# Copies of v and tau in DRAM: 16 KB apart instead of 4 KB

## The chip, the cores and the metric

The kernel runs on one core of a Trainium2 chip. The metric is the device time of one execution in microseconds; the time given for a kernel is the median of its runs. A core has five engines that work side by side, each with an instruction queue of its own: PE (TensorE, matrix products; PEld is its loading of weights), DVE (VectorE), ACT (ScalarE), POOL (GpSimd) and SP (SyncE, which here issues every DMA). DMAs move data between DRAM (HBM) and the on-chip memory SBUF; 16 DMA engines carry them. Everything is in 32-bit floats.

## The reference, cut to what matters

An image batch `x` of 4 x 64 channels x 256 x 256 goes through four layers. Layers 0, 2 and 3 are long convolutions with separable filters that small networks make; layer 1 works on Haar coefficients, and it alone uses `v` and `tau`:

```python
def conv_layer(x, ...):                    # layers 0, 2, 3
    hx, hy = filter_net_x(z), filter_net_y(z)
    y = causal_conv2d(x, outer(hx, hy))    # by FFT in the reference
    return y + x * bias

def layer_1(x, v, conv_w, tau):            # v, tau: (2, 1, 1, 256, 256)
    f1 = haar2d(x)
    acc = 0
    for i in range(2):
        f3 = f1 * v[i]
        f4 = einsum('bchw,oc->bohw', f3, conv_w[i])
        acc += sign(f4) * relu(abs(f4) - tau[i])
    return haar2d(acc, inverse=True) + x
```

A value of `v[i]` or `tau[i]` belongs to one place of the 256 x 256 coefficients and is the same for all 64 channels and all images.

## The kernel before

The kernel works on two groups of two images. Phase A is layer 0 and the forward Haar transform; it leaves the coefficients in the DRAM tensors `coef`. Phase B is the mixing of layer 1; it reads `coef`, and leaves its result in `mixed`. Phase C is the inverse Haar transform and layers 2 and 3. The phases are interleaved: phase A of group 0 runs alone, phase A of group 1 beside phase B of group 0, phase C of group 0 beside phase B of group 1, and phase C of group 1 alone.

Phase B runs in 64 steps per group. In a step the 128 partitions are 2 halves of 64 channels, and each half holds 2 rows of coefficients (`W = 2 * N = 512` values). The tiles for `v` and `tau` hold for each partition both branches `i` (2 x 512 values, 4 KB), and within a half all 64 channels hold the same values. So a load spreads one 4 KB row over 64 partitions. The kernel keeps `COPIES = 8` copies of every such row in DRAM, and each copy is read by 8 partitions:

```python
COPIES = 8
...
    taus = dram.tile([C, 2, COPIES, 2, W], F32, tag="taus", name="taus")
...
        def load(s):                                   # phase B, step s
            ...
            d["f"] = bp.tile([P, NB, W], F32, tag="ft", ..., bufs=4)
            for rows, f in step_of(coef[grp], s, d["f"]):      # 2 DMAs, 64 rows of 4 KB each
                nc.sync.dma_start(f, rows)
            for name, src in (("v", v), ("tau", taus)):
                t = d[name] = bp.tile([P, 2, W], F32, tag=name, ..., bufs=3)

                at = src.offset + s * 4 * W * COPIES
                flat = bass.AP(src.tensor, at, [[2 * W, 2 * COPIES], [0, C // COPIES], [1, 2 * W]])
                nc.sync.dma_start(t.rearrange("p e w -> p (e w)"), flat)
```

The source of a load is 16 rows (2 halves x 8 copies), each 4 KB after the one before it, each read 8 times. `v` is an input that is already laid out with its copies. `tau` is first scaled on the chip, and then written 8 times into the DRAM tensor `taus`:

```python
    def copy_tau(k):
        tau_sb = thresholds[1]                          # [128, 4, N] in SBUF
        for i in range(2):
            to = bass.AP(taus.tensor, taus.offset + (k * 2 + i) * W, [[2 * W * COPIES, P], [1, W]])
            nc.sync.dma_start(to, tau_sb[:, 2 * i : 2 * i + 2].rearrange("p h k -> p (h k)"))
...
    rest += [lambda k=k: copy_tau(k) for k in range(COPIES)]
```

`rest` is a list of preparations that is dealt out between the pieces of phase A of group 0; `copy_tau` comes last in it. In the same stretch SP issues, round by round, the images `x` of the next rounds and the filter matrices `tx` and `ty`:

```python
        def piece(t, j):                                # phase A, round t
            ...
            if j == 0:
                ...
                filters(t + 2)                          # tx, ty: 6 DMAs
            ...
                if j == 2 * BLOCKS + 1:
                    load(t + 2)                         # x: 1 MB, bufs=3
```

A step of phase B on one branch `i` goes through all the engines: PE makes the product `f` from `ft` and the mixing weights (L595), DVE multiplies it by `v` into `x` (L610), ACT takes the sign and the magnitude (L614, L618), DVE subtracts `tau` (L621) and applies the threshold (L624), and POOL adds to `gt` (L636 to L640), which is stored to `mixed` (L645).

Of the kernel before, what the change touches and what calls it, by code (L numbers as in the profile page):

```python
# [41 lines left out]
F32 = mybir.dt.float32  # L42
# [5 lines left out]
P = 128  # L48
B, C, N = 4, 64, 256
# [12 lines left out]

COPIES = 8

GROUPS = 2
NB = B // GROUPS
CI = 4 // NB
# [7 lines left out]
W = 2 * N  # L75
# [3 lines left out]

IMAGES = (GROUPS, NB, ROUNDS, CI, BLOCKS, ROW, N)  # L80
TO_ROUNDS = (0, 2, 1, 5, 3, 4, 6)
# [10 lines left out]
def conv_haar_kernel(  # L92
    ctx: ExitStack, tc: tile.TileContext, x, zT, w1, wbd, cols, decay, wo_first, decay_first, bias, forward, inverse, wcol, wrow, pack, v, tau, out
):
    nc = tc.nc
# [3 lines left out]
    dram = ctx.enter_context(tc.tile_pool(name="dram", bufs=1, space=DRAM))  # L99
# [3 lines left out]
    def coefficients(name):  # L103
        return dram.tile([CI, STEPS // 2, PAIR], F32, tag=name, name=name)

    coef = [coefficients(f"coef{g}") for g in range(GROUPS)]
    mixed = [coefficients(f"mixed{g}") for g in range(GROUPS)]
    filt = [dram.tile([P, REPEATS, PERIOD], F32, tag=f"filt{l}", name=f"filt{l}") for l in range(NL)]

    taus = dram.tile([C, 2, COPIES, 2, W], F32, tag="taus", name="taus")  # L110


    def pool(name, bufs, stack=ctx, **kw):
# [157 lines left out]
    def copy_tau(k):  # L271
        tau_sb = thresholds[1]
        for i in range(2):
            to = bass.AP(taus.tensor, taus.offset + (k * 2 + i) * W, [[2 * W * COPIES, P], [1, W]])
            nc.sync.dma_start(to, tau_sb[:, 2 * i : 2 * i + 2].rearrange("p h k -> p (h k)"))

    first_x = [load_x(0)]
    forward_sb = const.tile([P, ROW], F32, tag="forward", name="forward_sb")
# [15 lines left out]
    rest += [lambda l=l, q=q, k=k: spread(l, q, k) for l in (1, 2) for q in range(4) for k in thirds]  # L294
    rest.append(scale_tau)
    rest += [lambda k=k: copy_tau(k) for k in range(COPIES)]

    TILES = [(r, c) for r in range(2) for c in range(2)]
# [128 lines left out]
    def phase_a():  # L427


        total = GROUPS * ROUNDS  # L430
        st = [dict() for _ in range(total)]
# [97 lines left out]
    def phase_b(grp):  # L529
# [7 lines left out]
        def step_of(ap, s, images):  # L537

            n = NB * W
            by_e = images.rearrange("(m e) b w -> e m (b w)", e=CI)  # L540
            at = [ap.offset + (e * STEPS // 2 + s // 2) * PAIR + s % 2 * P // CI * n for e in range(CI)]
            return [(bass.AP(ap.tensor, at[e], [[n, P // CI], [1, n]]), by_e[e]) for e in range(CI)]

        def load(s):
            if s >= STEPS:
                return
            d = st[s]
            d["f"] = bp.tile([P, NB, W], F32, tag="ft", name=f"ft_{grp}_{s}", bufs=4)
            for rows, f in step_of(coef[grp], s, d["f"]):
                nc.sync.dma_start(f, rows)  # L550
            for name, src in (("v", v), ("tau", taus)):
                t = d[name] = bp.tile([P, 2, W], F32, tag=name, name=f"{name}_{grp}_{s}", bufs=3)

                at = src.offset + s * 4 * W * COPIES
                flat = bass.AP(src.tensor, at, [[2 * W, 2 * COPIES], [0, C // COPIES], [1, 2 * W]])
                nc.sync.dma_start(t.rearrange("p e w -> p (e w)"), flat)

        def four(name, at, b):
# [89 lines left out]
        def piece(u, j):  # L648

            s, i = divmod(u, 2)  # L650
            if j == 0:
                if u < units:
                    multiply(u)
                if 0 < u <= units:
                    less(u - 1)
                if 1 < u <= units + 1:
                    add(u - 2)
            elif j == 1:
                if u + 1 < units:
                    mix(u + 1)  # L660
                if u < units:
                    sign(u)
                if 0 < u <= units:
                    threshold(u - 1)
                if i == 0 and s > 0:
                    load(s + 2)
            else:
                if u < units:
                    magnitude(u)
                if i == 0 and s < STEPS:  # L670
                    exchange(s)
                if i and s > 0:

                    if s == 2:
                        part()
                        store(0)
                    if s > 1:
                        store(s - 1)

        def start():  # L680
            mixers.append(bp.tile([P, P], F32, tag="mix", name=f"mix_{grp}", bufs=1))
            nc.sync.dma_start(mixers[0], pack)
            for s in range(3):
                load(s)
# [7 lines left out]
    def phase_c():  # L692


        total = GROUPS * ROUNDS
        alone = total - ROUNDS
# [273 lines left out]
```

## Time and profile before

| what | value |
|---|---|
| time, median of 3 runs | 2849.76 us (2846.62 to 2851.04) |
| span of the profiled run | 2849.9 us |
| PE busy | 2429.2 us, 85% of the span |
| POOL busy | 1947.6 us, 68% |
| DVE busy | 1582.2 us, 56% |
| ACT busy | 1427.8 us, 50% |
| read from and written to HBM | 413.12 and 215.35 MB |

The profile is of one execution. Its page gives busy times by engine and in 40 slices, the chain of waits that ended last, the costliest groups of instructions by source line, and the DMA issues; the same trace can be asked for stretches of time. Lines such as L307 are lines of the kernel. `out<-in` names what an instruction or a DMA writes and reads: `v<-in_v` is the load of `v`, `tau<-taus` that of `tau`, `taus<-tau_sb` the writing of a copy. Two lines of the page show how the DMA engines' work is spread over the 40 slices of the span:

```profile
DMA  5668887989989998666888888887885444444432
GB/s 156 219 212 262 239 283 245 274 280 283 277 268 294 280 286 276 207 186 195 257 263 244 270 259 240 257 258 230 259 245 184 146 145 149 142 158 134 158 118 93
```

Each digit is the mean busy share of the 16 DMA engines in tenths in one slice of 71 us, and below it stands what they moved. Phase B of group 0 lies in slices 7 to 16, that of group 1 in slices 19 to 30.

### The profile page before, as it was taken

How to read it: one execution, taken by the hardware profiler on the slowest of the kernel's cores; microseconds unless marked ns; L12 is line 12 of the kernel's file. 1: busy time of each engine (PE TensorE's matmuls, PEld its weight loads, DVE VectorE, ACT ScalarE, POOL GpSimd, SP SyncE). 2: the span in 40 equal slices, each digit the busy share in tenths (PEclk: the TensorE clock that was granted, in tenths of full speed). 3: DMA queues.
4: the chain of work that ended last, by engine and by line, in shares of the span. 5: the costliest groups of instructions: out<-in, count | busy, mean ns of one | idle time of the engine just before them, and what ended most of it. 6: DMA issues, size and time to landing. Idle time of an engine off the chain costs nothing.

```text
span 2849.9 us, 120142 instructions
## 1 busy us (share of the span) xinstructions
PE 2429.2 (85%) x53276; PEld 1931.0 (68%) x53276; DVE 1582.2 (56%) x1779; ACT 1427.8 (50%) x2361; POOL 1947.6 (68%) x2422
## 2 busy tenths in 40 slices
PE   6999998667677676769888888888889999999999
PEld 5777776444444454547676767676667888888888
DVE  2353336777677777527776767676763333333333
ACT  1222224666656566426675666675763333333332
POOL 2787777977778787648777777776765555555561
PEclk9999999988988888879999999999999999999999
DMA  5668887989989998666888888887885444444432
GB/s 156 219 212 262 239 283 245 274 280 283 277 268 294 280 286 276 207 186 195 257 263 244 270 259 240 257 258 230 259 245 184 146 145 149 142 158 134 158 118 93
DMA packets 243773, 636.31 MB, mean 223 GB/s; under 512 B 43174, under 2 KB 125767, under 8 KB 227128
## 3 DMA queue, kind: packets, MB, share of 16 engines
q1 hardware_dynamic: 243256, 628.64, 71.5%
q8 instruction: 419, 6.86, 1.0%
q14 instruction: 98, 0.80, 0.1%
HBM read 413.12 MB, written 215.35 MB: 221 GB/s over the span
## 4 chain that ended last, share of the span: by engine, by line
PE 40%; DMA 23%; DVE 9%; ACT 5%; POOL 4%; issue 3%; SPq 3%; DVEq 0%; ACTq 0%; POOLq 0%
PE c1c L307 8%; PE c2r L307 8%; PE c2c L307 7%; PE c1r L307 6%; DMA ft<-coef 6%; DMA v<-in_v 4%; DMA tau<-taus 4%; PE f L595 3%; PE c0ps L319 3%; DMA x<-in_x 3%; DVE a L621 2%; DMA mixed<-gt 2%; DVE x L610 2%; DMA g<-mixed 2%; PE a2ps L307 1%
## 5 line engine op out<-in xcount | busy, mean ns | idle before, releaser
L392 POOL TENSOR_TENSOR i<-i,g 128x16 f32<-128x16 f32 x744 | 394.5, 550 | 489.3 <-ACT g L375 476.6
L595 PE MATMUL f<-ft,mix 64*64 64x512 f32 x2048 | 341.3, 687 | 262.2 <-DMA ft<-coef 180.5
L610 DVE TENSOR_TENSOR x<-f,v 128x1024 f32<-128x1024 f32 x256 | 312.0, 1219 | 267.0 <-PE f L595 140.4
L307 PEld LDWEIGHTS a1ps<-tx,x 64*64 64x64 f32 x8192 | 322.5, 142 | 121.5 <-issue 61.7
L307 PE MATMUL a1ps<-tx,x 64*64 64x192 f32 (+3 forms) x8192 | 354.2, 315 | 34.6 <-issue 11.2
L614 ACT ACTIVATE m<-x 128x1024 f32<-128x1024 f32 x256 | 272.0, 1063 | 209.9 <-DVE x L610 151.7
L307 PEld LDWEIGHTS c2r<-tx,cy 64*64 64x64 f32 x8192 | 307.6, 137 | 92.0 <-ACT ch L745 53.9
L307 PEld LDWEIGHTS c1c<-ty,ch 64*64 64x64 f32 x8192 | 300.9, 133 | 90.2 <-ACT ch L745 53.1
L307 PEld LDWEIGHTS a2ps<-ty,ay 64*64 64x64 f32 x8192 | 308.1, 140 | 70.8 <-issue 44.3
L307 PE MATMUL c2r<-tx,cy 64*64 64x256 f32 (+3 forms) x8192 | 341.6, 306 | 11.8 <-ACT ch L745 6.5
L307 PE MATMUL c1c<-ty,ch 64*64 64x192 f32 (+3 forms) x8192 | 330.3, 299 | 22.8 <-issue 12.7
L307 PE MATMUL a2ps<-ty,ay 64*64 64x256 f32 (+3 forms) x8192 | 340.8, 311 | 8.5 <-issue 7.8
L621 DVE TENSOR_TENSOR a<-a,tau 128x1024 f32<-128x1024 f32 x256 | 313.8, 1226 | 60.9 <-ACT a L618 60.5
L618 ACT ACTIVATE a<-x 128x1024 f32<-128x1024 f32 x256 | 264.8, 1034 | 162.3 <-DVE m L624 161.7
L307 PE MATMUL c1r<-tx,z 64*64 64x64 f32 (+3 forms) x8192 | 329.9, 302 | 12.5 <-ACT g L375 6.8
L307 PEld LDWEIGHTS c1r<-tx,z 64*64 64x64 f32 x8192 | 306.8, 136 | 49.8 <-issue 28.8
L636 POOL TENSOR_TENSOR gt<-gt,m 128x1024 f32<-128x1024 f32 x128 | 303.1, 2368 | 44.9 <-DVE m L624 41.8
L745 ACT COPY ch<-c1r 128x512 f32<-128x512 f32 x256 | 137.2, 588 | 390.5 <-PE c1r L307 390.1
L471 DVE SCALAR_TENSOR_TENSOR x<-x,bias_sb,a2ps 128x512 f32<-128x512 f32 x256 | 179.4, 742 | 268.2 <-PE a2ps L307 243.1
L307 PE MATMUL c2c<-ty,ch 64*64 64x192 f32 (+3 forms) x8192 | 319.3, 298 | 9.2 <-issue 9.2
L624 DVE SCALAR_TENSOR_TENSOR m<-a,m 128x1024 f32<-128x1024 f32 x256 | 313.0, 1223 | 22.1 <-DVE a L621 0.5
L307 PEld LDWEIGHTS c2c<-ty,ch 64*64 64x64 f32 x8192 | 300.5, 134 | 32.3 <-issue 18.4
(71 smaller groups left out, 3193.1 us busy)
## 6 DMA issues: line engine op xcount, KB each, us to landing
coef<-f SPq DMA_DIRECT2D x256, 256.0 KB, 4.1
ft<-coef SPq DMA_DIRECT2D x256, 256.0 KB, 6.8
v<-in_v SPq DMA_DIRECT2D x128, 512.0 KB, 7.5
tau<-taus SPq DMA_DIRECT2D x128, 512.0 KB, 8.5
mixed<-gt SPq DMA_DIRECT2D x256, 256.0 KB, 7.2
g<-mixed SPq DMA_DIRECT2D x256, 256.0 KB, 5.9
x<-in_x SPq DMA_DIRECT2D x63, 1024.0 KB, 8.5
out<-o SPq DMA_DIRECT2D x63, 1024.0 KB, 5.0
```

The source lines that it names most:

```text
L307: nc.tensor.matmul(ps[r][half(c), j % 2, k * ROW :], data[half(r), c, k, bass.ts(j, ROW)], t(r, c)[:, : N - k * ROW], start=k == 0, stop=k ...
L319: nc.tensor.matmul(ps[r][half(c)].rearrange("p h k -> p (h k)"), matrix[half(r)], pairs(r, c).rearrange("p h k -> p (h k)"), start=True, s ...
L392: engine.tensor_tensor(to, s, d, op)
L471: nc.vector.scalar_tensor_tensor(to, old, bias_sb[:, c : c + 1], ps, ALU.mult, ALU.add)
L595: nc.tensor.matmul(un[u]["f4"][half(q), b, :], mixers[0][half(r), bass.ts(i, C)], st[s]["f"][half(r), b], start=True, stop=True, tile_posi ...
L610: nc.vector.tensor_tensor(un[u]["x"], un[u]["f4"], both(u, "v"), ALU.mult)
L614: nc.scalar.activation(un[u]["m"], un[u]["x"], AF.Sign)
L618: nc.scalar.activation(un[u]["a"], un[u]["x"], AF.Abs)
L621: nc.vector.tensor_tensor(un[u]["a"], un[u]["a"], both(u, "tau"), ALU.subtract)
L624: nc.vector.scalar_tensor_tensor(un[u]["m"], un[u]["a"], 0.0, un[u]["m"], ALU.max, ALU.mult)
L636: nc.gpsimd.tensor_tensor(st[s]["g"], st[s]["g"], m, ALU.add)
L745: later(lambda y=y, ps=ps: nc.scalar.copy(y, ps))
```

## The change

The rows of four steps are put between two copies: `taus` and `v` go from (step, half, copy, row) to (step / 4, half, copy, step % 4, row). A load reads the same 16 rows as before, but they stand `FAR * 4 KB = 16 KB` apart. The aim is quicker loads of `v` and `tau`, by another placing of what the 16 DMA engines read at one time. `v` is laid out so before the launch. `taus` is written on the chip, and its rows no longer lie at one distance from partition to partition; so `copy_tau` writes every copy in 16 DMAs of 16 rows instead of 2 DMAs of 128 rows.

```diff
+FAR = 4
...
-    taus = dram.tile([C, 2, COPIES, 2, W], F32, tag="taus", name="taus")
+    taus = dram.tile([C // FAR, 2, COPIES, FAR, 2, W], F32, tag="taus", name="taus")
...
     def copy_tau(k):
         tau_sb = thresholds[1]
         for i in range(2):
-            to = bass.AP(taus.tensor, taus.offset + (k * 2 + i) * W, [[2 * W * COPIES, P], [1, W]])
-            nc.sync.dma_start(to, tau_sb[:, 2 * i : 2 * i + 2].rearrange("p h k -> p (h k)"))
+            n = FAR * 2 * W
+            for far in range(FAR):
+
+                for q in range(2):
+                    at = taus.offset + (q * COPIES + k) * n + (far * 2 + i) * W
+                    to = bass.AP(taus.tensor, at, [[2 * COPIES * n, C // FAR], [1, W]])
+                    rows = tau_sb[2 * far + q : P : 2 * FAR, 2 * i : 2 * i + 2]
+                    nc.sync.dma_start(to, rows.rearrange("p h k -> p (h k)"))
...
-                at = src.offset + s * 4 * W * COPIES
-                flat = bass.AP(src.tensor, at, [[2 * W, 2 * COPIES], [0, C // COPIES], [1, 2 * W]])
+                n = 2 * W
+                at = src.offset + (s // FAR * 2 * COPIES * FAR + s % FAR) * n
+                flat = bass.AP(src.tensor, at, [[FAR * n, 2 * COPIES], [0, C // COPIES], [1, n]])
...
-        "v": f(np.repeat(v[:, :, None], COPIES, axis=2)),
+
+        "v": f(np.repeat(v.reshape(C // FAR, FAR, 2, 2, W).transpose(0, 2, 1, 3, 4)[:, :, None], COPIES, axis=2)),
```

## The prediction

> **What bounds the kernel now.** I read the table by stage first, because the share of busy time on the page averages stages that have different limits. The stretches are: layer 0 of the first two images alone (370 to 420 us, a sample of it), mixing of group 0 beside layer 0 of group 1 (455 to 1150), mixing of group 1 beside layers 2 and 3 of group 0 (1290 to 2130), and layers 2 and 3 of group 1 alone (2130 to the end).
>
> ```profile
> core 0: us, PE busy (x) PEld busy (x) DVE busy (x) ACT busy (x) POOL busy (x), PEclk, DMA share, GB/s
> 370.00:420.00 50.00, 48.28 (x1166) 38.67 (x1158) 19.83 (x29) 13.90 (x26) 38.28 (x65) 1.00 0.79 279
> 455.00:1150.00 695.00, 491.43 (x8063) 319.08 (x8056) 514.40 (x488) 431.60 (x579) 547.07 (x607) 0.87 0.92 279
> 1290.00:2130.00 840.00, 724.41 (x15615) 579.40 (x15611) 595.54 (x601) 561.56 (x899) 623.33 (x639) 0.96 0.84 249
> 2130.00:2850.00 720.00, 706.06 (x18532) 628.26 (x18523) 248.46 (x352) 267.08 (x583) 381.05 (x525) 0.99 0.44 143
> ```
>
> In the first and last rows PE is busy 97 and 98% of the time: TensorE bounds them. In the row from 455 no engine is over 79% (POOL 547.07 of 695.00), but the 16 DMA engines are busy 92% of it: that stage is bound by transfers. In the row from 1290 PE has 86%, DMA 84%: a mixture. Only these two middle stages load v and tau. The chain of waits, asked for each of the two, says the same.
>
> ```profile
> by line: DMA ft<-coef 14.1%; DMA v<-in_v 14.0%; DMA x<-in_x 12.3%; DMA tau<-taus 12.1%; DVE x L610 5.1%; DVE a L621 5.1%; issue 4.5%; PE f L595 3.5%; DVE x L471 3.3%; DMA mixed<-gt 3.0%; PE a2ps L307 2.8%; DVE m L624 2.8%; DMA coef<-f 2.1%;
> ```
>
> ```profile
> by line: PE c1c L307 8.9%; DMA ft<-coef 7.9%; PE f L595 7.5%; PE c2r L307 7.5%; issue 6.1%; PE c2c L307 5.2%; DMA tau<-taus 5.0%; PE c1r L307 4.7%; DMA g<-mixed 4.6%; DMA mixed<-gt 4.3%; DMA v<-in_v 3.6%; DVE a L621 2.9%; DVE x L610 2.7%; A
> ```
>
> In the first line the DMA entries add to 57.6% of the stage (14.1 + 14.0 + 12.3 + 12.1 + 3.0 + 2.1), 26.1% of it v and tau themselves. In the second they add to 25.4% (7.9 + 5.0 + 4.6 + 4.3 + 3.6); much of the rest is PE. Next, the page's list of DMA issues, to see whether v and tau are slow for their size:
>
> ```profile
> ft<-coef SPq DMA_DIRECT2D x256, 256.0 KB, 6.8
> v<-in_v SPq DMA_DIRECT2D x128, 512.0 KB, 7.5
> tau<-taus SPq DMA_DIRECT2D x128, 512.0 KB, 8.5
> x<-in_x SPq DMA_DIRECT2D x63, 1024.0 KB, 8.5
> ```
>
> Landing times hold queueing, so they don't tell. The packet records of the trace do: each has a start, a size and a duration. I dealt the packets out to the DMAs by size in order of issue (a few at the borders between two DMAs fall to the wrong one) and took the mean duration in each stage. A 4 KB packet took, from 455 to 1150: v 281 ns, tau 249 ns, ft 193 ns (median 159), mixed stores 168, coef stores 166. From 1290 to 2130: v 285, tau 256, ft 180, mixed loads 206. So 159 ns is what a 4 KB packet takes undisturbed, and v and tau take 1.6 to 1.8 times that all through their 128 packets, while ft, issued just before them into the same kind of tile, does not. Per DMA engine, v and tau cost 139 + 123 = 262 us of the about 625 us I could deal out in the first stage, and 139 + 125 = 264 us in the second.
>
> [...]16 times 4096 B in 159 ns is 412 GB/s, while v at 281 ns makes 233 and tau at 249 makes 263.[...]
>
> **The change, part by part.** *Loads of v and tau.* Same 256 DMAs, same 512 KB, same 128 packets of 4 KB, same order on every engine; only the distance between the 16 source rows goes from 4 to 16 KB. If the distance is the cause, a packet falls to about ft's 193 ns. Each step loads both, so per step and engine it is 8 x (281 + 249) = 4.24 us now and 8 x 2 x 193 = 3.09 us then: 1.15 us less, times 64 steps = 74 us of DMA time from 455 to 1150. In the second stage 8 x (285 + 256 - 2 x 193) x 64 = 79 us. At 165 ns, which stores have now, it would be 102 and 108 us.
>
> How much of that reaches the end? In the first stage DMA time is 0.92 x 695 = 639 us; 639 - 74 = 565, and at the same 92% the stage would last 614 us, 81 less. But then POOL with 547 us would be at 89% and DVE with 514 at 84%, and their waits on each other no longer hide, so I take three quarters of the 81, 60 us (at 165 ns 111 us would go, and POOL would be past 93%: 75). In the second stage PE needs 724 of 840 us, so no more than 116 can go; DMA was 25% of the chain against 58%, so I take the same share of each saved us times 25/58, about 0.43 x 79 = 34, and call it 35 us (45 at 165 ns). Together 95 us, or 120 in the better case.
>
> *Writing the copies of tau.* This is the price. taus was written by 16 DMAs of 128 rows; with four steps' rows between the copies a partition step of 8 is needed, so it becomes 8 x 2 x 4 x 2 = 128 DMAs of 16 rows, 32 KB each. The instruction streams differ in nothing else. They fall between 367 and 420 us, where the SP queue looks like this (start, duration, what):
>
> ```profile
> 384.56 0.33 SPq L136 DMA_DIRECT2D x<-in_x  x1
> 384.94 2.64 SPq L149 DMA_DIRECT2D tx<-filt  x4
> 387.68 1.18 SPq L149 DMA_DIRECT2D ty<-filt  x2
> 388.90 1.20 SPq L275 DMA_DIRECT2D taus<-tau_sb  x2
> 390.20 2.96 SPq L488 DMA_DIRECT2D coef<-f  x4
> 393.21 2.01 SPq L275 DMA_DIRECT2D taus<-tau_sb  x2
> 395.80 0.33 SPq L136 DMA_DIRECT2D x<-in_x  x1
> ```
>
> One round of layer 0 takes 11.2 us (from one x load to the next), of which SP issues for some 10.4. The 16 taus issues take 12.4 us in all (sums of these lines over the stretch), 0.33 us for the shortest, as the x load does, and about 0.6 where they wait. SP also waits for earlier DMAs before it issues later ones that have nothing to do with them, as two lines of its waits from 455 on show:
>
> ```profile
> SPq L149 <- DMA v<-in_v: 30.4, 20, 2.0
> SPq L645 <- DMA tau<-taus: 26.5, 16, 3.2
> ```
>
> The built program's waits say why: DMAs take turns at eight semaphores, so at most eight are in flight. A small DMA lands in about 3 us (the quickest taus in 2.9), so 128 of them come at 3/8 = 0.37 us or more each; with the issue I take 0.40 us. That is 128 x 0.40 = 51 us in place of 12.4: 39 us more on SP. The stretch absorbs 7.6 us that SP now waits there for DVE, and the lead of x: it is issued 11.9 us before its first matmul (384.56 to 396.47) and lands in 6.5, which leaves 5.4. 39 - 7.6 - 5.4 = 26 us, and PE, at 97%, can't catch up before 455. So about +26 us of PE standing idle for x and the filters. The bytes are the same and the 112 more completion writes per engine of some 10 ns cost about 1 us.
>
> Sum of the case I hold most likely: -60 - 35 + 26 = -69 us, 2781 us. In the better case -75 - 45 + 26 = -94.
>
> **The rivals.** *The distance is not the cause; the repeated reading is.* [...]only 64 KB differ in a 512 KB load. For it: ft, mixed and x read every row once and are quicker, and the 1 KB row that all partitions read at the start (wrow) took 62 ns a packet against 48 for the different rows of decay. Against it: [...]v and tau differ by 32 ns although both repeat alike, so the place matters. Then packets stay at about 265 ns and only the +26 remain: 2876 us.
>
> *The sides of SBUF collide.*[...] Against it: ft and the loads of mixed write every other partition of their tiles[...] and their median is 159. Time then as in the first rival.
>
> *16 KB is worse than 4 KB,*[...] I give this little: +60 us or more.
>
> *The gain is hidden by the next bound.* POOL at 79%, DVE at 74% stand close behind DMA; if a step of mixing is a chain through PE, DVE, ACT and POOL rather than a flow, half of the 95 us goes: -47 + 26 = -21, 2829 us.
>
> *Issue is dearer than I think.* At 0.6 us each the 128 writes take 77 us, 52 rather than 26 us reach PE, and the likely case shrinks to -43 us, 2807.
>
> **Range and chances.** I give the distance about 0.65 to be the cause in full, 0.15 in part, 0.2 for one of the rivals without a gain. The likely and better cases lie at 2781 and 2756, with the hidden gain or the dear issue at 2807 to 2829, no gain at 2876. Weighted, I put the middle at 2784 us and the range at 2730 to 2876. Faster by over 2% means under 2793: 0.55. Within 2%: 0.39. Slower by over 2% (above 2907) needs slower packets as well as the stall: 0.06.
>
> **What the changed profile would show.** Right: v and tau packets near 190 ns or less; the first mixing stage some 60 us shorter with a DMA share under 92% and POOL near 88%; the waits of x and f on v, tau and ft shrunk; 128 taus issues that fill SP from 367 on, and PE idle before the first matmuls of layer 0 on x or tx, for 20 to 30 us in all. Wrong: v and tau packets still over 240 ns (the distance is not the cause); packets quicker but the stage as long (the bound is a chain of engines); no idle PE around 370 to 455 (SP had more room than I counted), or idle PE of 50 us or more (the issue is dearer).

## The result and the profile after

| | before | after |
|---|---|---|
| time, median | 2850.4 us (2846.62 to 2851.7) | 2917.8 us (2912.54 to 2923.06) |
| ratio after to before, 95% interval | | 1.0239 (1.0217 to 1.0260) |
| span of the profiled run | 2849.9 us | 2921.3 us |
| issues of taus on SP, number and sum | 16, 10.3 us | 128, 82.7 us |
| first load of v issued at | 454.4 us | 513.3 us |
| first mixing stage, from its first to its last load of tau | 703.3 us | 707.5 us |
| second mixing stage, likewise | 853.0 us | 864.7 us |

The change makes the kernel 2.4% slower. Of the 71.4 us between the two spans, 58.9 lie before the first load of v, that is in the stretch in which the copies of tau are written, and some 16 in the two mixing stages. The table by stage of the kernel after shows the same; its stretches are the writing of taus, the two mixing stages, and the end. In these tables each engine has its busy time, with the number of its instructions in brackets; the last three columns are the granted TensorE clock, the busy share of the DMA engines and what they moved in GB/s.

```profile
core 0: us, PE busy (x) PEld busy (x) DVE busy (x) ACT busy (x) POOL busy (x), PEclk, DMA share, GB/s
365.50:513.00 147.50, 93.15 (x2014) 77.85 (x2006) 30.83 (x45) 22.94 (x43) 66.12 (x112) 0.79 0.44 151
513.00:1221.00 708.00, 508.11 (x8100) 323.83 (x8096) 516.37 (x492) 434.20 (x583) 552.79 (x611) 0.86 0.90 276
1326.00:2190.00 864.00, 731.42 (x15619) 585.43 (x15614) 593.05 (x608) 562.09 (x902) 618.98 (x634) 0.95 0.83 245
2190.00:2921.00 731.00, 717.26 (x18797) 637.75 (x18787) 259.15 (x363) 276.18 (x598) 390.61 (x537) 1.00 0.45 146
```

Read the last columns of the first row: the DMA engines are busy 44% of it and PE 63% (93.15 of 147.50). Neither bounds the stretch; before, PE was busy 97% of the part from 370 to 420 us. The two mixing rows have nearly the same busy times and DMA shares as before: nothing has become quicker there. The chain of waits by line, asked for the two mixing stages of the kernel after:

```profile
by line: DMA v<-in_v 19.5%; DMA ft<-coef 11.6%; DMA x<-in_x 8.0%; DMA tau<-taus 7.0%; DMA mixed<-gt 5.6%; DVE x L619 5.2%; DVE a L630 4.9%; DMA coef<-f 4.7%; issue 4.1%; DVE m L633 3.1%; DVE x L479 2.7%; POOL f L365 2.3%; POOL fw L363 2.2%;
```

```profile
by line: DMA ft<-coef 10.1%; DMA tau<-taus 9.9%; PE c1c L315 7.9%; issue 6.3%; PE f L604 5.6%; PE c2r L315 5.6%; DMA v<-in_v 5.4%; SPq L151 5.3%; DMA g<-mixed 5.2%; PE c2c L315 5.1%; DMA mixed<-gt 3.2%; PE c1r L315 3.1%; DVE x L619 2.9%; DV
```

v alone is now 19.5% of the first stage against 14.0, and in the second an issue of SP has 5.3% (the filters, L151; the same issue, L149, had 1.7% before). The page's list of DMA issues of the kernel after:

```profile
ft<-coef SPq DMA_DIRECT2D x256, 256.0 KB, 6.7
v<-in_v SPq DMA_DIRECT2D x128, 512.0 KB, 8.2
tau<-taus SPq DMA_DIRECT2D x128, 512.0 KB, 8.7
x<-in_x SPq DMA_DIRECT2D x63, 1024.0 KB, 8.2
taus<-tau_sb SPq DMA_DIRECT2D x128, 32.0 KB, 1.9
```

v lands in 8.2 us in the median instead of 7.5, tau in 8.7 instead of 8.5. The packet records, dealt out as in the prediction (all packets of both stages now), say: v 284 ns in the mean against 283, tau 244 against 252. **The distance between the copies has not made the packets quick.** What did change is SP. Its queue in the stretch of the writes (start, duration, what):

```profile
397.50 10.08 SPq L283 DMA_DIRECT2D taus<-tau_sb  x16
407.68 0.53 SPq L138 DMA_DIRECT2D x<-in_x  x1
408.25 2.46 SPq L151 DMA_DIRECT2D tx<-filt  x4
410.80 1.18 SPq L151 DMA_DIRECT2D ty<-filt  x2
412.02 11.24 SPq L283 DMA_DIRECT2D taus<-tau_sb  x16
423.37 3.21 SPq L496 DMA_DIRECT2D coef<-f  x4
426.63 10.08 SPq L283 DMA_DIRECT2D taus<-tau_sb  x16
```

Sixteen issues take 10.08 us, which is 0.63 us each, again and again; the sum over 128 is 82.7 us. Waiting for earlier DMAs isn't what sets this pace: in the trace every DMA tells its landing on the same one of eight semaphores as the eighth before it (2773 of 2773), so with eight in flight one of them has 8 x 0.63 = 5.0 us until its turn comes again, and a copy lands in 1.9 us in the median (last line of the list above). The chain of waits, asked for 370 to 512 us, puts 41.4% of that stretch on these issues (SPq L283) and 15.6% on the loads of `x`. A round of layer 0 now waits for its `x`, because `x` stands behind two such blocks in the queue. PE's timeline in the same stretch (start, duration, what; in brackets the idle time before it and what ended it):

```profile
413.00 7.39 PE L315 MATMUL a1ps<-tx,x 64*64 64x256 f32 x126 [18.64 <-issue]
...
442.29 6.43 PE L315 MATMUL a1ps<-tx,x 64*64 64x256 f32 x126 [14.95 <-DMA x<-in_x]
...
461.48 7.05 PE L315 MATMUL a1ps<-tx,x 64*64 64x256 f32 x126 [5.82 <-DMA x<-in_x]
...
490.00 6.47 PE L315 MATMUL a1ps<-tx,x 64*64 64x256 f32 x126 [14.54 <-issue]
```

These are the first matmuls of four rounds. Each begins 5.2 to 5.5 us after the issue of its own `x` (407.68 to 413.00 in the two listings above), although before the change `x` was issued 11.9 us ahead. Where the bracket says "issue", the wait was for the same load, only not put down to it. The four idle times add to 53.95 us.

### The profile page after: what moved, and what is told of

Its sections match the earlier page's. It is cut to its first block, busy times and chain, and to the rows that moved or that the text cites. A ratio compares the mean times of both kernels' runs of the same rounds, so it can differ in the third digit from the quotient of the medians.

```text
span 2921.3 us, 120246 instructions
## 1 busy us (share of the span) xinstructions
PE 2452.3 (84%) x53276; PEld 1948.6 (67%) x53276; DVE 1581.1 (54%) x1779; ACT 1426.9 (49%) x2361; POOL 1947.7 (67%) x2422
## 4 chain that ended last, share of the span: by engine, by line
PE 41%; DMA 27%; DVE 9%; POOL 8%; SPq 8%; issue 4%; ACT 3%; DVEq 0%; ACTq 0%; POOLq 0%
PE c1c L315 8%; PE c2r L315 7%; PE c2c L315 7%; DMA v<-in_v 6%; PE c1r L315 6%; DMA ft<-coef 6%; DMA tau<-taus 5%; DMA x<-in_x 4%; PE a1ps L315 3%; PE c0ps L327 3%; PE a2ps L315 3%; POOL fw L363 3%; POOL f L365 3%; DMA mixed<-gt 2%; SPq L151 2%
## 5 line engine op out<-in xcount | busy, mean ns | idle before, releaser
L315 PEld LDWEIGHTS a1ps<-tx,x 64*64 64x64 f32 x8192 | 333.3, 148 | 174.8 <-issue 114.4
L315 PE MATMUL a1ps<-tx,x 64*64 64x256 f32 (+3 forms) x8192 | 366.6, 325 | 81.5 <-issue 38.3
L315 PE MATMUL c1r<-tx,z 64*64 64x192 f32 (+3 forms) x8192 | 329.2, 303 | 13.7 <-DMA tx<-filt 7.6
L315 PE MATMUL c2c<-ty,ch 64*64 64x192 f32 (+3 forms) x8192 | 325.4, 301 | 13.6 <-issue 13.5
```

Of the source, the lines that this page charges most:

```text
L315: nc.tensor.matmul(ps[r][half(c), j % 2, k * ROW :], data[half(r), c, k, bass.ts(j, ROW)], t(r, c)[:, : N - k * ROW], start=k == 0, stop=k ...
```

## The experiments

Each was timed on one chip in turn with the kernel before; the ratio is to that. The other columns are from one profiled run each: when the first load of v is issued, and how long each mixing stage lasts from its first to its last load of tau. Packet times are of 4 KB packets of v and tau, mean over both stages, with the median after the stroke.

| kernel | ratio (95%) | first v load | mixing stages, us | v, ns | tau, ns |
|---|---|---|---|---|---|
| before | 1 | 454.4 | 703 and 853 | 283/275 | 252/254 |
| after | 1.0239 (1.0217 to 1.0260) | 513.3 | 708 and 865 | 284/264 | 244/248 |
| near_128_writes | 1.0227 (1.0194 to 1.0260) | 509.4 | 701 and 854 | 282/273 | 250/255 |
| far_16_writes | 1.0052 (1.0036 to 1.0068) | 449.2 | 705 and 861 | 283/262 | 243/246 |
| v_far_only | 1.0127 (1.0086 to 1.0167) | 443.7 | 722 and 877 | 301/268 | 244/248 |
| v_36kb_apart | 0.9982 (0.9967 to 0.9998) | 452.2 | 695 and 838 | 273/265 | 246/246 |
| v_own_rows | 0.9943 (0.9920 to 0.9966) | 449.5 | 688 and 849 | 275/267 | 248/252 |
| v_128_rows | 0.9845 (0.9794 to 0.9896) | 440.2 | 674 and 829 | 214/159 | 253/252 |
| v_by_parity | 0.9933 (0.9910 to 0.9956) | 443.7 | 698 and 836 | 253/238 | 250/242 |
| v_plain_halves | 1.0126 (1.0102 to 1.0150) | 446.4 | 715 and 876 | 291/282 | 292/285 |
| v_plain_parity | 0.9852 (0.9822 to 0.9881) | 446.0 | 685 and 832 | 209/159 | 257/248 |
| copies_16 | 0.9480 (0.9447 to 0.9513) | 464.1 | 631 and 760 | 201/159 | 188/159 |
| copies_32 | 0.9447 (0.9419 to 0.9475) | 459.6 | 624 and 761 | 201/159 | 184/159 |
| far_copies_16 | 0.9554 (0.9519 to 0.9589) | 468.6 | 647 and 775 | 222/159 | 181/159 |

**Is the loss the issue of the writes, or the placing?** The first two kernels each have one half of the change.

near_128_writes keeps the rows 4 KB apart and writes them in 128 DMAs:

```diff
-            to = bass.AP(taus.tensor, taus.offset + (k * 2 + i) * W, [[2 * W * COPIES, P], [1, W]])
-            nc.sync.dma_start(to, tau_sb[:, 2 * i : 2 * i + 2]...)
+            for first in range(8):
+                at = taus.offset + (first * COPIES * 2 + k * 2 + i) * W
+                to = bass.AP(taus.tensor, at, [[2 * W * COPIES * 8, P // 8], [1, W]])
+                nc.sync.dma_start(to, tau_sb[first:P:8, 2 * i : 2 * i + 2]...)
```

> The rows stand 4 KB apart as before, but tau's copies are written by 128 DMAs of 16 rows. If issue is the whole loss: phase B begins about 59 us later than before and the time is 2908 to 2918 us. If the placing brings 12 to 16 us of the loss: 2902 to 2908 us. If the distance of the copies mattered at the writing (16 rows 256 KB apart), the issue of one would not be about 0.6 us here as well.

Measured: 2907.85 us, 1.0227, nearly the whole loss. The SP queue in its timeline:

```profile
392.75 10.08 SPq L277 DMA_DIRECT2D taus<-tau_sb  x16
402.93 0.52 SPq L136 DMA_DIRECT2D x<-in_x  x1
403.49 2.46 SPq L149 DMA_DIRECT2D tx<-filt  x4
406.05 1.17 SPq L149 DMA_DIRECT2D ty<-filt  x2
```

The same 10.08 us for sixteen issues, with the copies 4 KB apart: the number of DMAs sets it, not the distance of the copies. 128 issues took 80.8 us, and phase B began 55 us later. (Within one of these DMAs the 16 rows stand 256 KB apart in both kernels, so these two don't compare that distance.)

far_16_writes has the placing of the change, but one DMA writes a whole copy for one half, 64 rows of 4 KB (both branches of a row lie side by side in DRAM):

```diff
-            for far in range(FAR):
-                for q in range(2): ...                      # 16 DMAs a copy
+        for q in range(2):                                  # 2 DMAs a copy
+            at = taus.offset + (q * COPIES + k) * n
+            to = bass.AP(taus.tensor, at, [[2 * COPIES * n, C // FAR], [2 * W, FAR], [1, 2 * W]])
+            nc.sync.dma_start(to, tau_sb[q:P:2].rearrange("p h k -> p (h k)"))
```

> The rows of v and tau stand 16 KB apart as in the changed kernel, but tau's copies are written by 16 DMAs of 64 rows of 4 KB. If the issue of 128 small DMAs is the whole loss and the placing does nothing: 2845 to 2860 us, v and tau packets about 280 and 245 ns, phase B begins at about 455 us. If the placing itself costs the 12 to 16 us that phase B took longer in the changed kernel: 2862 to 2868 us. If the placing helps and the stall hid it: below 2835 us.

Measured: 2856.84 us, 1.0052. Phase B begins at 449.2 us, so the stall is gone with the small DMAs (16 issues took 10.5 us); what is left is a small loss, and no gain. The waits for v, from the waits of this kernel and of the next one (total us, times, longest; 122.2 us before):

```profile
DVE x L615 <- DMA v<-in_v: 189.3, 56, 8.8
```

```profile
DVE x L612 <- DMA v<-in_v: 228.6, 63, 9.7
```

v_far_only places v alone 16 KB apart, tau and its writing as before.

> Kernel before, but v alone stands 16 KB apart; tau and its writing as before. The placing of both cost 0.5% with 8 copies (and v waits grew from 122 to 189 us). If it is the placing of v that costs: ratio 1.004 to 1.007, landing of v about 7.9 us in place of 7.5. If it is tau's, or the other form of tau's writes: ratio 0.998 to 1.002.

Measured: 1.0127, more than expected, in the direction of the first theory: 16 KB costs v. In all four kernels with v at 16 KB the slow end of its packets is longer: 95 of 100 are under 521 (after), 520, 613 and 553 ns, against 447 before (429 in copies_16, with which the fourth, far_copies_16, compares), while the median is no higher. The loads of v land later too, in 8.2, 7.9, 8.2 and 7.1 us in the median against 7.5 before and 6.6 in copies_16. That this costs more alone than together with tau, and that tau itself lost nothing at 16 KB, I can't explain; it is left open.

**If not the distance, what makes a packet of v and tau take 250 to 285 ns?** First the rival of repeated reading. v gets 9 rows for each of its 16 groups in DRAM, and reads 8 of them (v_own_rows) or the first one 8 times (v_36kb_apart):

```diff
+                    at = src.offset + s * 2 * COPIES * 9 * 2 * W
-                flat = bass.AP(src.tensor, at, [[2 * W, 2 * COPIES], [0, C // COPIES], [1, 2 * W]])
+                    flat = bass.AP(src.tensor, at, [[9 * 2 * W, 2 * COPIES], [2 * W, C // COPIES], [1, 2 * W]])
# v_36kb_apart:                                                    ... [0, C // COPIES] ...
```

> Kernel before, but every partition has a row of its own of v (the same values): 16 groups of 8 rows, 4 KB from row to row[...]; 512 KB differ in each load; tau as before. If reading one row eight times is what makes the packets slow: v packets fall from about 281 to 160 to 195 ns, tau stays near 250, DMA time falls by about 8 x 100 ns x 128 = 100 us, and the time falls by 40 to 80 us, to 2770 to 2810. If something else does (the side of SBUF, the shape of the DMA): v stays at 260 to 290 ns and the time within 10 us of before.

> As v_own_rows in DRAM[...]. If repetition is the cause: v packets about 280 ns, time as before (2845 to 2860). If the distance is the cause and 16 KB was only too little or too even: v packets under 220 ns and time under 2820.

Measured: v 275 and 273 ns, 0.9943 and 0.9982, a gain of 0.6 and 0.2%, but not the one that either theory needs. With eight neighbouring partitions to a group, neither a row of its own for each partition nor a distance of 36 KB makes the packets quick. What v, tau and these kernels share is the shape: 16 groups of eight. The next kernel reads v in one plain block of 128 rows.

```diff
-                    flat = bass.AP(src.tensor, at, [[2 * W, 2 * COPIES], [0, C // COPIES], [1, 2 * W]])
+                    flat = bass.AP(src.tensor, src.offset + s * P * 2 * W, [[2 * W, P], [1, 2 * W]])
```

> Kernel before, but v is loaded as one plain block of 128 rows, one for each partition, 512 KB in one piece; tau as before. v_own_rows had different rows too, but in 16 groups of 8. If the groups[...] are what makes v slow[...]: v packets fall to 160 to 200 ns, some 40 us of DMA time in each mixing stage go, and the time falls by 30 to 70 us, to 2775 to 2815. If v is slow for any other reason (the order behind ft, HBM): v stays at 265 to 285 ns and the time near v_own_rows, 2820 to 2850.

Measured: v 214 ns with a median of 159, tau beside it unchanged, 0.9845. Against v_own_rows only the grouping differs (and one spare row in nine). Is it the grouping of the source, or the partitions that one DMA writes? Three kernels load v in two DMAs of 64 rows. The last two have plain rows: if the partitions are the cause, halves and parity differ; if only the grouping is, both are quick.

```diff
# v_by_parity: groups, even and odd partitions
+                    for e in range(2):
+                        flat = bass.AP(src.tensor, at, [[2 * W, 2 * COPIES], [0, C // COPIES // 2], [1, 2 * W]])
+                        nc.sync.dma_start(t[e:P:2]..., flat)
# v_plain_halves: plain rows, partitions 0 to 63 and 64 to 127
+                        at = src.offset + s * P * 2 * W + e * ROW * 2 * W
+                        flat = bass.AP(src.tensor, at, [[2 * W, ROW], [1, 2 * W]])
+                        nc.sync.dma_start(t[e * ROW : (e + 1) * ROW]..., flat)
# v_plain_parity: plain rows, even and odd partitions
+                        at = src.offset + s * P * 2 * W + e * 2 * W
+                        flat = bass.AP(src.tensor, at, [[4 * W, ROW], [1, 2 * W]])
+                        nc.sync.dma_start(t[e:P:2]..., flat)
```

> Kernel before, but v is loaded by two DMAs, one for the even and one for the odd partitions, as ft is; the same 16 rows 4 KB apart, each read four times by each DMA. If the shape of the destination is the cause and ft's is a good one: v packets 160 to 200 ns. If groups of rows on the source side are the cause whatever the destination: v stays at 250 to 285 ns. 128 more issues of 0.6 us on SP, which phase B has room for: time 2790 to 2830 in the first case, 2845 to 2865 in the second.

> v in plain rows of its own for every partition, in two DMAs of 64 rows: partitions 0 to 63, then 64 to 127. [...]v packets are 250 to 320 ns although source and shape are plain; time within 15 us of before. If only the grouped shape of the source is slow: v packets about 160 to 210 ns as in v_128_rows, time near 2795 to 2805.

> The same rows and the same number of DMAs as v_plain_halves, but one DMA takes the even and one the odd partitions[...]: v packets 160 to 210 ns, time 2790 to 2810, 30 us or more below v_plain_halves. If not: no difference between the two.

Measured: the two plain kernels issue the same number of DMAs and fetch the same rows in a step; halves give 291 ns (1.0126), parity 209 with a median of 159 (0.9852). Two things differ: the partitions that one DMA writes, and the rows that it reads, 64 in a row or every other one. The rows aren't the cause: in both kernels ft also reads 64 in a row, into every other partition, and takes 185 and 184 ns with a median of 159. So it is the partitions: **what limits here is the side of SBUF, 291 ns in halves against 209 in parity**. Their lines in the lists of DMA issues, halves first:

```profile
v<-in_v SPq DMA_DIRECT2D x256, 256.0 KB, 7.3
```

```profile
v<-in_v SPq DMA_DIRECT2D x256, 256.0 KB, 6.5
```

The halves cost 36 us by the ratio, more than expected. v_by_parity has the good partitions and the bad grouping, and v took 253 ns: the grouping of the source acts too (its time, 2825.33 us, is below what I expected with such packets). With all 16 engines at work, 16 x 4096 B in 291 ns make an estimated 225 GB/s for v in halves, in 283 ns 232 for v before, and in 209 ns 314 for v in parity. What joins the two causes is not shown: the packet records of the trace name neither the engine that carries a packet nor the partition that it writes. Halves against parity is shown, and so is 16 groups against plain rows.

**A better version.** If groups of eight make the packets slow, smaller groups may do so less. copies_16 has 16 copies, so 32 groups of four, and writes each copy of tau in one DMA; the placing is dense as before. Two outcomes stood open: quick packets if groups of four are small enough, packets as before if they are not.

```diff
-COPIES = 8
+COPIES = 16
-        for i in range(2): ...
+        to = bass.AP(taus.tensor, taus.offset + k * 2 * W, [[2 * W * COPIES, P], [1, 2 * W]])
+        nc.sync.dma_start(to, tau_sb.rearrange("p h k -> p (h k)"))
```

> 16 instead of 8 copies of v and tau, so 32 rows, each read by four partitions; tau's copies are written by 16 DMAs of 128 rows of 4 KB. [...]v and tau packets fall to 160 to 200 ns and the time to 2740 to 2800. [...]packets 250 to 285 ns, time 2835 to 2860.

Measured: 2693.35 us, 0.9480, beyond the expected range; v and tau at 201 and 188 ns, both with a median of 159. Its table by stage, for the two mixing stages:

```profile
core 0: us, PE busy (x) PEld busy (x) DVE busy (x) ACT busy (x) POOL busy (x), PEclk, DMA share, GB/s
464.00:1095.00 631.00, 481.96 (x8123) 309.92 (x8119) 518.91 (x493) 433.08 (x583) 550.16 (x608) 0.91 0.88 310
1200.00:1960.00 760.00, 708.27 (x15548) 580.43 (x15543) 587.81 (x604) 559.80 (x901) 615.94 (x632) 0.98 0.79 279
```

```profile
by line: issue 8.6%; DMA v<-in_v 7.9%; POOL f L356 7.6%; POOL fw L354 7.1%; DVE a L620 7.0%; DVE x L609 6.1%; POOL gt L635 5.8%; DMA ft<-coef 5.3%; DVE x L470 5.2%; DMA x<-in_x 4.6%; DMA tau<-taus 4.0%; DVE m L623 3.6%; POOL gt L639 3.0%; P
```

The first stage now moves 310 GB/s instead of 279 and lasts 631 us instead of 703. In its chain of waits, the last line above, the DMA entries shown add to 21.8%, against 57.6% before: POOL, DVE and DMA now take turns. In the second stage PE is at 93% (708.27 of 760.00), and TensorE is close to being the bound there.

copies_32 has 32 copies, and far_copies_16 has 16 copies that stand 16 KB apart, written by 32 DMAs.

> 32 copies, 64 rows each read by two partitions. [...]packets as with 16 copies (about 190 to 210 ns, median 159), and only the writing of 16 more copies is added, 16 x 0.6 = 10 us of issue and 8 MB: 2695 to 2720. If fewer repetitions help too: below 2685.

> 16 copies as in copies_16, but 16 KB apart as in the changed kernel, tau's copies written by 32 DMAs of 64 rows of 4 KB. If the distance never matters: 2693 plus up to 16 x 0.6 = 10 us for 16 more issues, 2690 to 2710. If the distance helps once the destination is not in the way: below 2680. If it costs, as it cost 15 us with 8 copies: 2710 to 2725.

Measured: 0.9447 (2690.06 us, a little under what I expected) and 0.9554. The interval of copies_32 overlaps with that of copies_16: the packets are as quick, and 16 copies already give what 32 do. With 16 KB the time is 2716.42 us, some 23 more than copies_16. The 16 more issues took 10.5 us of SP, and phase B began 4.5 us later (468.6 against 464.1); v at 222 instead of 201 ns fits a further cost. So even with quick packets the change's placing gives nothing.

## Why the prediction was wrong

**The bound: right.** The first mixing stage was bound by transfers, and slow packets of v and tau were the reason. copies_16 shows it: it saves 8 x (283 + 252 - 201 - 188) ns x 64 = 75 us of DMA time in each stage, and the stages became 72 and 93 us shorter. (The packets of ft, mixed and g became quicker as well, by 7, 6 and 16 ns, an estimated 7 and 15 us more of DMA time.)

**What reaches the end: too little.** I let through three quarters of the gain in the first stage (60 us of 81) and 0.43 of the DMA time saved in the second (35 us). In copies_16, which saves about the DMA time that I had assumed, 72 and 93 us arrived. The DMA share of the chain, 25%, was no measure of what a DMA saving is worth in the second stage. That is a mis-sized term, too, but it played no part in the miss, since there was no saving to pass on.

**The step that failed: "If the distance is the cause, a packet falls to about ft's 193 ns".** I gave 0.65 to the distance as the cause in full. It isn't: 284 and 244 ns after, 273 at 36 KB. I read ft's 159 ns as proof of a good distance in DRAM. At what distance the engines read at one time no trace shows, and ft differs from v in two more ways: its rows are plain, not grouped, and one DMA writes every other partition. I named "the sides of SBUF collide" as a rival and dropped it because the packets of ft, into every other partition, have a median of 159 ns. That argument didn't ask whether the shape of the source matters. v_by_parity and v_plain_parity, on the same partitions with and without groups, take 253 and 209 ns (median 238 and 159), and v_own_rows and v_128_rows, with a row of its own for each partition in both, 275 and 214: the grouping matters where the partitions are the same. How it does so is not shown. The rival of repeated reading fell too (275 ns against 273).

**The mis-sized term: the issue of the writes.** I took 0.40 us for each of 128; it was 82.7 / 128 = 0.65. I had taken the shortest issue, 0.33 us, and the eight DMAs in flight at 3 us each; but the small ones land in 1.9 us, and back to back an issue takes 0.587 us in the median. The rest of the sum comes out: 72.4 us more on SP, less the 13 us of slack that I counted (7.6 + 5.4), is 59.4, and phase B began 58.9 us later. So close an agreement is partly luck. My 12.4 us for the 16 issues held the short gaps between them; counted so, the writes rose by 76.9 us. And SP's wait for DVE up to the first load of v fell from 16.4 to 1.5 us, more than the 7.6 that I had read from a shorter stretch. "Issue is dearer than I think" was there as a rival, at 52 us, and so was idle PE of 50 us or more as its sign; with no gain from the packets that makes 2902 us. I put a loss of over 2% at 0.06 because it seemed to need slower packets as well as the stall; near_128_writes, with the stall and packets of 282 and 250 ns, lost 2.3% alone.

**The remainder.** I gave "16 KB is worse than 4 KB" little. Placing costs 0.5% (far_16_writes), some 15 us, enough for the 12.5 us that the late start leaves. But near_128_writes without it is at 1.0227, and its interval overlaps with that of the change: how much the placing adds beside the stall isn't resolved. So the sum of the change is some +59 from the issues, up to +15 from the placing, and nothing on the other side.

## What to carry to other kernels

When the packets of a load are slow, change source and destination one at a time before choosing a cure: the same rows into other partitions (halves against even and odd, with ft beside them reading 64 rows in a row) told here what no reading of addresses could. A load that spreads few rows over 128 partitions should not be cut into 16 groups, as far as these runs go: 32 groups of four took 188 to 201 ns a packet where 16 groups of eight took 252 to 283. And a layout that is cheap to read can be dear to write: count the DMAs on the queue that issues them, at the back-to-back price of some 0.6 us and not at that of a lone one (0.33 us for x).

## What the runs showed of the hardware that was not expected

An issue on SP takes about 0.59 us when others precede it closely, be it 32 KB in 16 rows (taus after, median 0.587), 256 KB in 64 rows (far_16_writes, 0.592) or in 128 rows (taus before, 0.584). An issue of x took 0.53 us right behind them (407.68 above) and 0.33 after a pause of the queue (384.56 in the prediction's list). The 128 small DMAs landed in 1.9 us in the median and took 0.587 us each to issue, and the issue was the bound.

A starved TensorE is also slower when its data come. After the idle times listed above the first 126 matmuls of a round took 6.43 to 7.39 us, against 4.67 for 124 of them in an undisturbed round before (385.24 us in its trace). The granted clock accounts for it: during these four bursts 0.61, 0.70, 0.64 and 0.70 of the full clock was granted, against 1.00 in the round before the change, and each duration times its clock gives 4.5 us. SP bound most of the stretch, but the last two bursts lie in the chain of waits that ended last, so an estimated 4 us of the later start (7.05 and 6.47 less 4.67 each) can be theirs.

tau's packets became slower in v_plain_halves (292 against 252 ns) although only v had changed. Its loads are issued right behind those of v (455.0 and 454.4 us for the first of each in the trace before), which may be one reason; the dealing out at the borders may be another. No run separates the two.
